# Layer 0 of a two-layer graph network: the weighted values of two source tiles as seven block products, each in its own PSUM bank

## The chip, the cores and the metric

One NeuronCore of a Trainium2 chip runs the whole program in one launch. The metric is device time in microseconds (us) from start to end of one execution. Engines are called as in the profile: PE (TensorE, its weight loads PEld), DVE (VectorE), ACT (ScalarE), POOL (GpSimd) and SP, whose queue issues most DMAs. Each engine takes its instructions in the written order, and what waits holds up all that stands behind it.

## The reference

Two layers over 4096 nodes with 512 features; `adj` is a 4096 x 4096 matrix of weights, about 1.6 % of them not zero. All arithmetic is float32.

```python
h = relu(layernorm(x))                       # layer 0
q, k, v = h @ Wq.T + bq, h @ Wk.T + bk, h @ Wv.T + bv
a = q @ k.T / sqrt(512) + adj + adj
x = x + softmax(a, axis=-1) @ v
h = relu(layernorm(x))                       # layer 1: 8 heads of 64 features
nX = a_ln * normalised(h @ W) + b_ln         # per head: mean and deviation over 64
kg = leaky_relu(at1 + at2.T, 0.2) * adj      # at1, at2: nX times a1, a2
y = softmax(where(adj != 0, kg, -32768)) @ nX + nX
x = x + elu(y)
```

## The kernel before

**Three phases.** The projections (layer norm, values `v`, queries times the key weights) fill the first 290 us. Layer 0's attention runs to about 2095 us. Layer 1 takes the rest. The change is in the first two.

**Tiles of layer 0.** Logits are held with sources on partitions and targets along the row. A *chunk* is 512 targets (`ic`, 8 of them), a *tile* one block of 128 sources by 512 targets (`jt`, 32 per chunk), and the loop handles a *pair* of tiles per round: 128 rounds, `s` counting tiles. In a round PE computes the scores of the next pair (s+2, s+3) and the weighted values of this one (s, s+1).

**Scores (`stage`, `product`, L740).** The scores of a pair are a 2 x 2 block matrix product, done with seven block products (Strassen's scheme in Winograd's form) of 128 x 256 outputs, each two matmuls deep, in four stages: stage 0 computes two products, stages 1 and 2 two each, stage 3 one. Their sums build up in three PSUM tiles, Z (one buffer) and X (two buffers). After each stage DVE adds Z or X onto the half tiles of `aT`, which hold the transposed adjacency (`add_part`, L748, 128x256 each, seven per pair); ACT takes exp of a whole tile in place (L753, after stages 2 and 3); POOL adds it onto `total`, the sum over sources (L758).

**Weighted values (`weighted`, L768).** For each tile and each of four blocks of 128 targets one matmul: 128 x 128 of the exponentials against 128 x 512 of `v`, accumulated over the 32 tiles of the chunk in four PSUM banks `acc0` to `acc3`. Eight per pair. PSUM has eight banks: four `acc`, two X, one Z, and one, `m`, that `small()` hands to the side jobs.

**Side jobs.** When a chunk ends, `chunk_end` divides its rows by their totals and adds `x`, and `make_ready` prepares them for layer 1 during the rounds of the next chunk: layer norm, four transposes per 128 rows (`turn`), the projection (`project`, four 512-column matmuls), deviations per head, attention coefficients, `sides` (small transposes) and `fours`. These jobs stand in a table `later`, keyed by step; the loop runs those that are due between the matmuls. In `m` they meet no score and no accumulator.

**Other work of a round.** DVE transposes two new adjacency tiles in 32 x 32 blocks (`swap`, L485) and writes mask and edge tiles for layer 1 (`for_layer_1`: `ng` L730, `gs` L732), which SP stores to DRAM. SP loads adjacency, hidden features (`hT`, `hS`) and, once per chunk, query tiles.

**Order.** All of this is put in program order by hand (`seq`); no scheduler moves it. Where one instruction needs another engine's result, or its buffer, the framework adds a semaphore wait; it tracks buffers by tile.

A round before, with PE's matmuls in this order: stage 0, `weighted` blocks 0 and 1, stage 1, blocks 2 and 3, side jobs, stage 2, three blocks of tile s+1, stage 3, the last block, side jobs. DVE's first swap and `for_layer_1` stand between the adds of stages 0 and 1, the second ones between those of stages 2 and 3.

Of the kernel before, what the change touches and what calls it, by code (L numbers as in the profile page):

```python
# [43 lines left out]
HUGE1 = 1e36  # L44

# [33 lines left out]
def fast_path(  # L79
# [50 lines left out]
    for t in (low0, high0):  # L130
        nc.vector.memset(t, 1.0)
# [4 lines left out]
    h_d = dram.tile([NS, P, KC, GC], F32, name="h_d")  # L136
    s_d = dram.tile([NS, P, 4, KC // 2, 2, P], F32, name="s_d")
    q_d = dram.tile([NI, P, KC, GC], F32, name="q_d")
    t_d = dram.tile([NI, P, 4, KC // 2, GC // 2], F32, name="t_d")
# [35 lines left out]
    def means(pool, rows, name):  # L175

        st = pool.tile([P, SB, 6], F32, name=f"{name}st", tag=f"{name}st", bufs=2)
        mv = pool.tile([P, SB, 2], F32, name=f"{name}mv", tag=f"{name}mv", bufs=2)
        for b in range(SB):
            seq(nc.vector.bn_stats(st[:, b, :], rows[b]))  # L180
            seq(nc.vector.bn_aggr(mv[:, b, :], st[:, b, :]))
        return mv
# [65 lines left out]
    def make_ready(ic, x1s, small, at_step, gap, last):  # L248

        n = SB * NH  # L250
# [5 lines left out]

        def features(b):
            return x1s[b].rearrange("p (h e) -> p h e", e=HD)

        def stats():  # L260
            state["mv"] = means(prep, x1s, "l")
# [19 lines left out]
        def turn():  # L281
            xn = state.pop("xn")
            m = small([P, KC, P])
            for k in range(KC):
                seq(nc.tensor.transpose(m[:, k, :], xn[:, ts(k, P)], ident))
            h1 = prep.tile([P, KC, P], F32, name="h1", tag="h1", bufs=1)
            seq(nc.scalar.activation(h1, m, AF.Relu))
            state["h1"] = h1

        def project():  # L290
            h1 = state.pop("h1")
            m = small([P, 2, GC] if last else [P, GC])
            y = m[:, 0, :] if last else m
            for k in range(KC):
                seq(nc.tensor.matmul(  # L295
                    y, h1[:, k, :], w1_sb[:, k].rearrange("p h e -> p (h e)"),
                    start=k == 0, stop=k == KC - 1,
                ))
            state["y"] = y
            if last:  # L300
                state["a"] = m[:, 1, 0 : 2 * NH]
                for k in range(KC):
                    seq(nc.tensor.matmul(
                        state["a"], h1[:, k, :], w1a_sb[:, k].rearrange("p e h -> p (e h)"),
                        start=k == 0, stop=k == KC - 1,
                    ))

        def keep_features(b):
            seq(nc.vector.tensor_copy(x1s[b], state.pop("y")))
            if last:  # L310
                seq(nc.vector.tensor_copy(
                    raw[:, b].rearrange("p e h -> p (e h)"), state.pop("a")
                ))
# [8 lines left out]

        def flat(t):
            return t.rearrange("p b h -> p (b h)")
# [11 lines left out]

        def root():
            v = flat(var)
            seq(nc.gpsimd.tensor_scalar(v, v, 1.0 / (HD - 1.0), 1e-30, ALU.mult, ALU.max))
            r = inverse_root(nc.gpsimd, prep, v, n, "s")  # L340
            seq(nc.gpsimd.tensor_mul(r, r, v))
            seq(nc.gpsimd.tensor_scalar_add(r, r, STD_EPS))
            state["r"] = r

        def inverse():
            seq(nc.vector.reciprocal(flat(var), state.pop("r")))
# [55 lines left out]
        def sides(b):  # L402
            r = ic * SB + b
            m = small([P, 4, P])
            for kind in range(4):
                seq(nc.tensor.matmul(
                    m[:, kind, :], parts[:, b, kind].rearrange("p h r -> p (h r)"),
                    ident_b, start=True, stop=True,
                ))
            zc = prep.tile([P, 4, P], BF16, name="zc", tag="zc", bufs=2)  # L410
            seq(nc.scalar.copy(zc, m))
            for g in range(2):
# [4 lines left out]
            nc.sync.dma_start(out=z1_d[:, :, ts(r, P)], in_=zc[:, 2:4, :])  # L417

        def fours():
# [3 lines left out]
            seq(nc.tensor.transpose(m, at1s.rearrange("p b h -> p (b h)"), ident))  # L423
# [6 lines left out]
        else:  # L430
            at_step(0, stats)
        at_step(0 if last else 1, deviations)
        for b in range(SB):
            d = (0 if last else 2) + gap * b
            at_step(d, norm, b)
            at_step(d + 1, turn)
            at_step(d + 2, project)
            at_step(d + 2, keep_features, b, late=True)
            at_step(d + 3, square, b)
            at_step(d + 3, variance, b, late=True)  # L440
            if last:
# [3 lines left out]
        if last:  # L445
            at_step(d + 6, ats)
            at_step(d + 6, split)
            for b in range(SB):
                at_step(d + 8 + b, sides, b)
                at_step(36 + 32 * b, own, b)  # L450
            at_step(d + 11, fours)
        else:
            at_step(d + 4, root)
            at_step(d + 6, inverse)
            for b in range(SB):
                at_step(d + 7 + b, products, b)
                at_step(d + 8 + b, sums_of, b)
                at_step(d + 12 + b // 2, own, b)
                at_step(d + 13 + b, sides, b)
            at_step(d + 11, split)  # L460
            at_step(d + 16, fours)
# [6 lines left out]
    with tc.tile_pool(name="early", bufs=2) as early, tc.tile_pool(name="kv", bufs=1) as kv:  # L468
# [26 lines left out]
        def load_chunk(ic, queue):  # L495
            loaded = []
            for k in range(KC):
                qt = early.tile([P, GC], F32, name="qt", tag="qt", bufs=16)
                seq(queue.dma_start(out=qt, in_=q_d[ic, :, k, :]))
                loaded.append(qt)  # L500
            for e in range(4):
                qt = early.tile([P, GC], F32, name="qt", tag="qt", bufs=16)
                seq(queue.dma_start(out=qt, in_=t_d[ic, :, e].rearrange("p k i -> p (k i)")))
                loaded.append(qt)
            queries_of[ic] = loaded
# [3 lines left out]
        def side_b(ic, name):  # L509

            q = queries_of[ic]
            if name[0] == "B":
                return [q[2 * (int(name[1]) - 1) + k][:, ts(int(name[2]) - 1, H)] for k in range(2)]
            return [q[3 + int(name[1])][:, ts(k, H)] for k in range(2)]

        def side_a(sb, pair, name):

            h, sums = hidden_of[sb]
            if name[0] == "A":
                tile_ = 2 * pair + int(name[1]) - 1  # L520
                return [h[:, 2 * (int(name[2]) - 1) + k, ts(tile_, P)] for k in range(2)]
# [11 lines left out]
        def load_hidden(sb):  # L533
            for t, ap in zip(hidden_tiles(sb), (h_d, s_d)):
                flat = "p a b -> p (a b)" if ap is h_d else "p a b c d -> p (a b c d)"
                seq(nc.sync.dma_start(out=t.rearrange(flat), in_=ap[sb].rearrange(flat)))


        with tc.tile_pool(name="proj_c", bufs=1) as pc, tc.tile_pool(
# [10 lines left out]
            bv_sb = early.tile([P, D], F32, name="bv_sb", tag="qt", bufs=16)  # L550
# [18 lines left out]
            def hidden(sb, xt):  # L569
# [17 lines left out]
                for t, ap in ((h, h_d), (sums, s_d)):  # L587
                    flat = "p a b -> p (a b)" if ap is h_d else "p a b c d -> p (a b c d)"
                    seq(nc.sync.dma_start(out=ap[sb].rearrange(flat), in_=t.rearrange(flat)))

            def values_of(sb):
                for b in range(SB):
# [6 lines left out]
                    seq(nc.vector.tensor_add(v[:, sb * SB + b, :], pv, bv_sb))  # L599

# [3 lines left out]
            def queries(sb):  # L604
                qs = pc.tile([P, KC, GC], F32, name="qs", tag="qs", bufs=1)
                for o in range(KC):
# [10 lines left out]
                seq(nc.sync.dma_start(  # L617
                    out=q_d[sb].rearrange("p k i -> p (k i)"), in_=qs.rearrange("p k i -> p (k i)")
                ))
                t = [  # L620
                    prep.tile([P, KC // 2, H], F32, name="ts", tag="x1", bufs=SB) for _ in range(4)
                ]
# [7 lines left out]
                for e in range(4):  # L630
                    seq(nc.sync.dma_start(
                        out=t_d[sb, :, e].rearrange("p k i -> p (k i)"),
                        in_=t[e].rearrange("p k i -> p (k i)"),
                    ))

# [67 lines left out]
        with tc.tile_pool(name="attn", bufs=2) as work, tc.tile_pool(  # L703
# [6 lines left out]

            def small(shape):
                return psum.tile(shape, F32, name="m", tag="m", bufs=1)

            def load_residual(ic):
                rows_of[ic] = []
                for b in range(SB):
                    x1 = prep.tile([P, D], F32, name="x1", tag="x1", bufs=SB)
                    nc.sync.dma_start(out=x1, in_=x[ts(ic * SB + b, P), :])
                    rows_of[ic].append(x1)
# [30 lines left out]
            def exponent0(s):  # L750
                ic, jt = TILES[s]
                p = turned.pop(s)
                seq(nc.scalar.activation(p, p, AF.Exp, scale=2.0))  # L753
                if jt == 0:
                    totals[ic] = work.tile([P, GC], F32, name="total", tag="total", bufs=2)
                    seq(nc.gpsimd.tensor_copy(totals[ic], p))
                else:
                    seq(nc.gpsimd.tensor_add(totals[ic], totals[ic], p))  # L758
                probs[s] = p

            def weighted(s, b):
                ic, jt = TILES[s]
                if jt == 0 and b == 0:
                    sums[ic] = [
                        psum.tile([P, D], F32, name=f"acc{b}", tag=f"acc{b}", bufs=1)
                        for b in range(SB)
                    ]
# [904 lines left out]
```

## Time and profile before

| what | us |
|---|---|
| median of three runs (3783.66 to 3793.55) | 3793.2 |
| the profiled execution | 3789.07 |
| its span, first to last instruction | 3787.3 |
| PE busy over the span | 3648.9 (96 %) |
| DVE, POOL, ACT busy | 2534.2, 2056.7, 1726.2 |
| layer 0's attention, 290 to 2090 us: PE, DVE, POOL, ACT busy of 1800 | 1770.0, 1039.6, 633.2, 230.9 |

Busy time counts an engine's instructions from start to end, overlaps once. A row of a timeline gives start, duration, engine, line, operation, operands and count of merged instructions; in brackets stands idle time before it and what ended that. A float32 matmul appears as two instructions (4 for a block product two deep), and a matmul's recorded duration overlaps the next one's: the spacing of starts says what it costs.

### The profile page before, as it was taken

To read this page: it belongs to the slowest core of one execution; us is meant where nothing else is said; L and a number is where in the kernel's file an instruction comes from. 1 tells how busy PE (TensorE), PEld (TensorE's weight loads), DVE (VectorE), ACT (ScalarE), POOL (GpSimd) and SP (SyncE) were. 2 spreads that over 40 slices of the span, in tenths; PEclk is the share of its full clock that TensorE was granted. 3 is DMA by queue.
4 is the path that set the end of the run, shared out by engine and by line. 5 is a ranking of instruction groups with operands and counts; after the bars stand their busy time and mean duration, and the time that the engine had idled before them with its cause. 6 is when DMAs were issued, how large, how long until landed. Compare 5 with 4: busy or idle time off the path is not lost. (4 is left out here: it accounts for less than half of the span.)

```text
span 3787.3 us, 53732 instructions
## 1 busy us (share of the span) xinstructions
PE 3648.9 (96%) x19722; PEld 1747.0 (46%) x19722; DVE 2534.2 (67%) x3875; ACT 1726.2 (46%) x1501; POOL 2056.7 (54%) x1348
## 2 busy tenths in 40 slices
PE   8999999999999999999999689999999999999998
PEld 3446666666666666666666222223323232222222
DVE  5535556556565565656655458888888888888787
ACT  1000011111111111111111379899999999998897
POOL 3432224325252242523415468888888888877786
PEclk9999999999999999999999799999999999999999
DMA  6466766858668675676856788877788887888775
GB/s 201 181 212 190 201 182 192 213 160 225 174 191 226 181 217 163 200 212 182 220 150 183 160 197 212 211 208 209 208 211 205 211 210 205 210 206 204 196 209 153
DMA packets 623041, 746.18 MB, mean 197 GB/s; under 512 B 84848, under 2 KB 468272, under 8 KB 603312
## 3 DMA queue, kind: packets, MB, share of 16 engines
q1 hardware_dynamic: 614896, 717.69, 68.1%
q0 software_dynamic: 6480, 23.60, 3.5%
q8 instruction: 156, 2.56, 0.3%
q10 hardware_dynamic: 1392, 1.38, 0.1%
q14 instruction: 117, 0.96, 0.1%
HBM read 562.43 MB, written 172.23 MB: 194 GB/s over the span
## 5 line engine op out<-in xcount | busy, mean ns | idle before, releaser
L1030 POOL TENSOR_TENSOR t<-t,g 128x1024 f32<-128x1024 f32 x512 | 1223.3, 2399 | 341.1 <-DVE t L1024 228.5
L1049 PE MATMUL acc<-t,nX 128*64 128x512 f32 x4096 | 1008.8, 609 | 0.0
L1037 ACT ACTIVATE t<-t 128x2048 f32<-128x2048 f32 (+1 forms) x527 | 976.5, 1853 | 0.6 <-POOL t L1030 0.5
L768 PE MATMUL acc<-v,aT 128*128 128x512 f32 x2048 | 963.2, 593 | 0.0
L758 POOL TENSOR_TENSOR total<-total,aT 128x512 f32<-128x512 f32 x248 | 340.4, 1372 | 1064.0 <-ACT aT L753 1051.8
L1024 DVE SCALAR_TENSOR_TENSOR t<-u,at2m,r 128x512 f32<-128x512 f32 x1024 | 719.2, 744 | 248.6 <-issue 143.8
L753 ACT ACTIVATE aT<-aT 128x512 f32<-128x512 f32 x256 | 161.2, 630 | 1323.1 <-DVE aT L748 1301.0
L1033 DVE TENSOR_TENSOR t<-l,g 128x1024 f32<-128x1024 f32 x512 | 623.6, 1218 | 22.9 <-DMA g<-gT_d 20.1
L992 ACT ACTIVATE l<-l 128x1024 f32<-128x1024 f32 x512 | 516.3, 1008 | 179.9 <-PE l L986 128.1
L768 PEld LDWEIGHTS acc<-v,aT 128*128 128x128 f32 x2048 | 390.1, 190 | 274.1 <-issue 246.0
L1049 PEld LDWEIGHTS acc<-t,nX 128*64 128x64 f32 x4096 | 248.0, 136 | 457.7 <-issue 450.9
L748 DVE TENSOR_TENSOR aT<-aT,X 128x256 f32<-128x256 f32 x512 | 214.9, 420 | 288.5 <-PE X L740 285.4
L748 DVE TENSOR_TENSOR aT<-aT,Z 128x256 f32<-128x256 f32 x384 | 159.6, 416 | 306.4 <-PE Z L740 301.7
L732 DVE SCALAR_TENSOR_TENSOR gs<-ng,aT 128x512 f32<-128x512 bf16 x256 | 279.4, 1091 | 9.8 <-DMA gT_d<-gs 1.1
L740 PE MATMUL Z<-qt,hS 128*128 128x256 f32 x1024 | 265.6, 382 | 8.4 <-DVE aT L748 8.4
L740 PE MATMUL X<-qt,hT 128*128 128x256 f32 x1024 | 264.6, 381 | 0.5 <-DVE aT L748 0.5
L740 PE MATMUL X<-qt,hS 128*128 128x256 f32 x1024 | 263.6, 380 | 0.0
L740 PEld LDWEIGHTS Z<-qt,hS 128*128 128x128 f32 x1024 | 192.9, 191 | 131.7 <-issue 56.9
L976 PEld LDWEIGHTS <-z 6*128 6x128 bf16 x2048 | 52.7, 91 | 429.5 <-DVE t L1024 337.7
L986 PE MATMUL l<-z_left,z 64*64 64x512 bf16 x2048 | 202.7, 383 | 49.4 <-DVE t L1033 16.7
L740 PEld LDWEIGHTS X<-qt,hT 128*128 128x128 f32 x1024 | 195.4, 191 | 81.9 <-issue 55.0
L1006 PE MATMUL r<-nx,ident_b 64*64 64x512 bf16 x1024 | 209.7, 403 | 3.0 <-DMA nx<-nT_d 3.0
(180 smaller groups left out, 3559.9 us busy)
## 6 DMA issues: line engine op xcount, KB each, us to landing
g<-gT_d SPq DMA_DIRECT2D x128, 1024.0 KB
ag<-in_adj_dram SPq DMA_DIRECT2D x256, 256.0 KB
hT<-h_d SPq DMA_DIRECT2D x64, 1024.0 KB
hS<-s_d SPq DMA_DIRECT2D x64, 1024.0 KB
gT_d<-gs SPq DMA_DIRECT2D x256, 256.0 KB
nb<-nT_d SPq DMA_DIRECT2D x128, 512.0 KB
nx<-nT_d SPq DMA_DIRECT2D x256, 256.0 KB
nT_d<-ng SPq DMA_DIRECT2D x256, 128.0 KB
```

Source lines behind the costliest of these rows:

```text
L732: seq(nc.vector.scalar_tensor_tensor(gs, ng, G_MASKED / NEG_BIG, aT, ALU.mult, ALU.add))
L740: seq(nc.tensor.matmul(out, a, b, start=start and k == 0, stop=k == 1, skip_group_check=not start,))
L748: seq(nc.vector.tensor_add(p, p, part))
L758: seq(nc.gpsimd.tensor_add(totals[ic], totals[ic], p))
L768: seq(nc.tensor.matmul(sums[ic][b], probs[s][:, ts(b, P)], v[:, jt, :], start=jt == 0, stop=jt == NB - 1))
L992: seq(nc.scalar.activation(lefts[n], lefts[n], AF.Relu, scale=4.0))
L1006: seq(nc.tensor.matmul(out[first + 2 * r][ts(c, HD), :], ident_b[rows, rows], masks[r != c][rows, jt % JB, :], start=False, stop=True, ski ...
L1024: seq(nc.vector.scalar_tensor_tensor(t[:, 2 + e, :], u4[:, e, :], at2m[:, jt, h : h + 1], right[e], ALU.max, ALU.add))
L1030: seq(nc.gpsimd.tensor_mul(t[:, 2:4, :], t[:, 2:4, :], both_heads(n)))
L1033: seq(nc.vector.tensor_mul(logits[n][:, 0:2, :], lefts.pop(n), both_heads(n)))
L1037: seq(nc.scalar.activation(t, t, AF.Exp))
L1049: seq(nc.tensor.matmul(grp["acc"][hf][ts(e, HD), :], nX[jt // SB][:, jt % SB, hg * HG + 2 * hf + e, :], t[:, hf + 2 * e, :], start=jt == 0 ...
```

## The change

The weighted values of a pair become a 2 x 2 block product too, done with seven products of 128 x 256 blocks. Of `A` (the pair's exponentials, in halves of 256 targets) POOL forms four sums per pair (`pair_sums`), and three adds per pair keep the totals; of `B` (the values, in halves of 256 features) the sums are formed once, in the projections: one takes the place of a half of `v`, and three per pair go to DRAM (`vt_d`) and are loaded in each round (`load_sums`). Each product accumulates over the chunk in a bank of its own, M1 to M7, with two 128-target halves in it. At a chunk's end one ACT copy and ten DVE adds combine the seven banks, in steps (`end()`) spread over two rounds.

Seven banks leave one. It is the tile XZ: Z is its first half, X its second, and `small()` gives the side jobs the Z half. What a side job left there is cleared by ACT (`zeros`, 128 x 256) before or after, as the slot asks. Side jobs run in three slots of a round: slot 0 after stage 3 of the round before, slot 1 after stage 0, slot 2 after stage 2; the jobs are cut to half a bank (`turn` and `project` into two parts, `sides` into two).

PE's order in a round is now: slot 0, products 1 and 7, stage 0, slot 1, products 2 and 4, stage 1, product 5, stage 2, slot 2, products 6 and 3, stage 3.

The residual `x` is added by an accumulating DMA on POOL's queue; ACT divides the rows. Query factors are stored as seven tiles of 256 KB per chunk. A fifth test at the end of the program asks that in each column of statistics the largest row total be at most 256 times the smallest, or the general path runs.

```diff
+            xz = psum.tile([P, 2, H], F32, name="XZ", tag="XZ", bufs=1)
             def small(shape):
-                return psum.tile(shape, F32, name="m", tag="m", bufs=1)
+                slot["used"] = True
+                if slot["n"] == 2:
+                    zeros()
+                m = xz[: shape[0], 0, 0 : math.prod(shape[1:])]
...
             def exponent0(s):
                 seq(nc.scalar.activation(p, p, AF.Exp, scale=2.0))
-                    seq(nc.gpsimd.tensor_add(totals[ic], totals[ic], p))
+            def pair_sums(s):
+                seq(nc.gpsimd.tensor_sub(s3, a11, a21))
+                seq(nc.gpsimd.tensor_add(s1, a21, a22))
+                seq(nc.gpsimd.tensor_sub(s2, s1, a11))
+                seq(nc.gpsimd.tensor_sub(s4, a12, s2))
...
+                    for t, a in ((total[0], a11), (total[0], a12), (total[1], s1)):
+                        seq(nc.gpsimd.tensor_add(t, t, a))
...
-            def weighted(s, b):
-                seq(nc.tensor.matmul(
-                    sums[ic][b], probs[s][:, ts(b, P)], v[:, jt, :], start=jt == 0, stop=jt == NB - 1
-                ))
+            def weighted(s, *which):
+                for i in which:
+                    a, b = factors[s][i]
+                    for u in range(2):
+                        seq(nc.tensor.matmul(
+                            sums[ic][i][:, u, :], a[:, ts(u, P)], b,
...
                 if n == 0:
-                    w["x"] = psum.tile([P, H], F32, name="X", tag="X", bufs=2)
-                    w["z"] = psum.tile([P, H], F32, name="Z", tag="Z", bufs=1)
+                    w["z"], w["x"] = xz[:, 0], xz[:, 1]
...
+                def divide(b):
+                    seq(nc.scalar.activation(
+                        x1s[b], x1s[b], AF.Identity, scale=rows_of[ic][:, b : b + 1]
+                    ))
+                def residual():
+                    seq(nc.gpsimd.dma_start(
+                        out=rows, in_=x[ts(ic, GC), :].rearrange("(b p) d -> p b d", p=P),
+                        accum_op=ALU.add,
+                    ))
+                    store_rows(ic, x1s)
...
+                parts_of_end = [
+                    then((copy, c11, m[1])),
+                    then((add, c22, c11, m[7])),
+                    then((add, c12, c11, m[5]), (add, c11, c11, m[2])),
+                    then((add, c21, c22, m[4]), (add, c22, c22, m[5])),
+                    then((add, c12, c12, m[6]), (add, c21, c21, m[6])),
+                    then((add, c22, c22, m[6]), (add, c12, c12, m[3])),
+                ]
+                at_step(s, 2, total_of_rows)
...
+                def hooks(n):
+                    slot.update(n=n, used=False)
+                    for f in later.pop(3 * (s // 2) + n, []):
+                        f()
+                    if n == 1 and slot["used"]:
+                        zeros()
...
+        for b in range(SB):
+            d = 8 + 6 * b
+            at_step(d, norm, b)
+            at_step(d + 1, turn, range(0, 2))
+            at_step(d + 2, turn, range(2, 4))
+            at_step(d + 3, project_half, b, 0)
+            at_step(d + 4, project_half, b, 1)
+            at_step(d + 4, square, b)
+            at_step(d + 5, variance, b)
+            at_step(d + 5, root_of, b)
...
+        for b in range(SB):
+            at_step(36 + 2 * b, sides, b, 0)
+            at_step(37 + 2 * b, sides, b, 1)
+            at_step(36 + 2 * b, own, b)
+        at_step(45, fours)
```

A step number counts three slots per round, from the first round of the next chunk.

## The prediction

> **What bounds the kernel now.** I read the busy table by stage first: in layer 0's attention (290 to 2090 us) PE is busy 1770 of 1800 us and the granted clock is 1.00. The list of PE's waits in that stretch holds 30 us in all, so the order of PE's matmuls sets the time. Then the timeline of PE alone, for one round without side jobs:
>
> ```profile
> 299.19 2.74 PE L768 MATMUL acc<-v,aT 128*128 128x512 f32 x6
> 301.77 1.03 PE L740 MATMUL X<-qt,hT 128*128 128x256 f32 x4
> 302.63 1.02 PE L768 MATMUL acc<-v,aT 128*128 128x512 f32 x2
> 303.49 1.03 PE L740 MATMUL Z<-qt,hT 128*128 128x256 f32 x4
> 304.35 1.03 PE L740 MATMUL X<-qt,hT 128*128 128x256 f32 x4
> 305.22 1.88 PE L768 MATMUL acc<-v,aT 128*128 128x512 f32 x4
> 306.93 1.03 PE L740 MATMUL Z<-qt,hS 128*128 128x256 f32 x4
> 307.80 1.03 PE L740 MATMUL X<-qt,hS 128*128 128x256 f32 x4
> 308.66 1.88 PE L768 MATMUL acc<-v,aT 128*128 128x512 f32 x4
> 310.38 1.03 PE L740 MATMUL Z<-qt,hS 128*128 128x256 f32 x4
> 311.24 1.03 PE L740 MATMUL X<-qt,hS 128*128 128x256 f32 x4
> 312.10 2.74 PE L768 MATMUL acc<-v,aT 128*128 128x512 f32 x6
> ```
>
> A round is 312.10 - 299.19 = 12.91 us, with no gap. Four 128x256 instructions (one block product) take 0.86 us from start to start, two of 128x512 also 0.86: the time goes by columns, 0.215 us per 256, and the weight loads hide. So 7 products (6.02) and 16 instructions of 512 columns (6.88) make 12.90.
>
> What a wait costs shows where PE does wait, in the first pair, before any weighted values fill the gaps:
>
> ```profile
> 285.84 1.03 PE L740 MATMUL X<-qt,hS 128*128 128x256 f32 x4
> 286.04 0.42 DVE L748 TENSOR_TENSOR aT<-aT,Z 128x256 f32<-128x256 f32 x1 [1.03 <-PE Z L740]
> 286.55 0.63 ACT L753 ACTIVATE aT<-aT 128x512 f32<-128x512 f32 x1 [55.58 <-DVE aT L748]
> 286.90 0.42 DVE L748 TENSOR_TENSOR aT<-aT,X 128x256 f32<-128x256 f32 x1 [0.44 <-PE X L740]
> 287.38 1.13 PE L740 MATMUL X<-qt,hT 128*128 128x256 f32 x4 [0.51 <-DVE aT L748]
> 288.35 1.03 PE L740 MATMUL Z<-qt,hT 128*128 128x256 f32 x4
> ```
>
> X's four end, by spacing, at 286.70; DVE starts its add 0.20 later, needs 0.42, and 0.06 after it PE starts again, on a group that takes 0.97 in place of 0.86, its first load being bare. PE end to DVE: 0.20. DVE end to PE: 0.06 + 0.11 = 0.17. ACT follows DVE by about 0.1.
>
> **Part 1, the products.** 16 instructions of 512 columns become 28 of 256 per round: 6.88 to 6.02, 0.86 less. X and Z show that 256-column instructions with a new weight each keep 0.215. 128 rounds: **-110 us**.
>
> **Part 2, one bank for Z and X.** The built program shows that waits on XZ are for the tile: the first product of each stage waits for the last add of the stage before, and the first add for the stage's last product. What must fit between two stages is 0.20, two adds, 0.17. Adds on different tiles start 0.33 apart where both are ready (296.12 and 296.45 in the timeline), on the same half 0.52 (293.45 and 293.97). Stages 0 to 1: 0.20 + 0.52 + 0.42 + 0.17 = 1.31, under two products (1.72). Stages 2 to 3: 1.12 under 1.72. Stage 3 to the next 0: one add, 0.79 under 1.72. Stages 1 to 2: 0.20 + 0.33 + 0.42 + 0.17 = 1.12 over product 5 alone, 0.86: PE stands 0.26 per round, 127 times: **+33**. The bounds are 0.2 and 0.5.
>
> **Part 3, the side jobs.** Before, `m` was free when they came; PE's waits for them sum to 13.5 us, all in `fours`. Now each writes the Z half directly after a stage, and PE, in order, waits for that stage's adds with nothing in between. The program has 84 such places in slot 0, 49 in slot 1 and 50 in slot 2: 26 per chunk in seven chunks, and the last `total_of_rows` stands after no stage but is counted too.
> - Slot 0, after stage 3: 0.20 + 0.42 + 0.17 = 0.79 if DVE is free. DVE comes from the second swap, `ng` and `gs` (0.70 + 0.43 + 0.69, with gaps 1.90), which starts 0.95 after stage 2's end; stage 3 ends 2.58 after it, so the add is ready at 2.78 and DVE free at 2.85, later where POOL's first subtraction holds it. I take 0.9: 84 x 0.9 = 76. Bounds 0.75 and 1.3.
> - Slot 1: two adds on one half, 1.31: 49 x 1.31 = 64. Bounds 1.2 and 1.6.
> - Slot 2: the clearing stands behind the exp: 0.20 + 0.42 + 0.10 + 0.63, then the clearing. No row has 128x256 on ACT; PSUM rows of 512 and 1024 columns take 0.59 and 1.01, so 0.82 ns a column and about 0.38. With 0.17 that is 1.90: 50 x 1.90 = 95. Bounds 1.1 (if exp does not come first) and 2.4.
> The matmuls of the jobs are as many columns as before. The jobs' readers (ACT or DVE, 0.4) hide under the two products that follow. Sum **+235**.
>
> **Part 4, DVE late.** DVE gets its first swap block after stage 0's adds, free 0.20 + 0.94 + 1.90 = 3.04 after stage 0; stage 1's adds are due at 3.64. A slack of 0.6 covers it, except where `variance` (0.68 and its wait) stands before: 28 rounds late by some 0.8, **+22**. POOL and DVE disturb each other: `gs` takes 0.69 alone and 1.64 beside a POOL add (mean 1.08). POOL's new work is seven adds of 256 columns per round; from 0.27 at 32 columns and 1.265 at 512, an estimate of 0.73 each, 5.1 us in place of 2.7. They run mostly before DVE's block; 0.15 us in 70 rounds, **+10** (0 to 30).
>
> **Part 5, the queues.** In round 0 of a chunk POOL's DMA of the residual waits for four ACT divisions (0.80 each, as `xn`), about 4.6 us after stage 2, and takes 0.9 to issue (L1093's rows); the next pair's first subtraction stands behind it, 0.73, so product 7 is due at 3.4 and gets its input at 6.5: 7 x 3.1 = **+22** (0 to 30). SP issues one more load per round (0.35 us of 12) and eight row stores that wait for that DMA; the edge stores behind them have a round's time. Traffic per round goes from 2.3 to 2.55 MB at 68 % share: hidden, 0 to 15 if not. A chunk's ten adds (0.69 each) are spread, and only the pair before stage 1 is late by 0.8: **+8** in all. The residual of the last chunk behind layer 0: **+5**. Projections: 64 POOL operations more (47 us on an engine busy 106 of 290): **+3**, up to 15. Layer 1 unchanged.
>
> **Sum.** -110 + 33 + 235 + 22 + 10 + 22 + 8 + 5 + 3 = +228, on the profiled 3789: 4017, and 4 more for the median of the runs: **4021**. The low ends (25; 63 + 59 + 55; 22; zeros) give +114, so 3907; the high ends (64; 109 + 78 + 120; 22 + 30 + 30; 38) give +381, so 4174.
>
> **A rule of the skill.** Idle clocks are the question here. The trace has PE idle 6.40 us at 280.77, and the 256-column instructions after it start 0.43 apart for some 3.5 us; after 1.96 us idle at 293.92 they keep 0.215. My longest regular stall is 1.9 us, so by the rows the clock holds. The Trainium skill ("TensorE: Matmul & The Clock Gate", section "A second HAM failure mode: psum-queue depth-cycling") says instead that a PE that micro-idles often between groups while it cycles through PSUM falls back to half clock again and again. By it, as an estimate, one window of 3.4 us at half speed for each of 183 stalls would add some 310 us.
>
> **Rivals.**
> 1. *Faster.* The bank waits are covered, and only the products count: -110 + 33 + 16 = 3728 (3680 to 3770). It needs a mean side-job stall under (110 - 33 - 16) / 183 = 0.33 us, less than one add (0.42). In order behind a stage, with 0.20 and 0.17 around the add, I see no way. 0.06.
> 2. *Slower than forecast by DVE.* POOL's adds hold `ng` and `gs` in every round: with 1.52 and 1.64 (both are in the trace) DVE is free at 5.0 instead of 3.04, 1.35 late in the 78 rounds without a slot-1 job: +105, 4125 (4090 to 4200). For it: POOL's share doubles. Against: its operations are half as long, and end as DVE's block begins. 0.13.
> 3. *Nothing.* Stalls about half as long (the jobs' waits being shared with waits that stand anyway): within 0.3 %, 0.02.
> 4. *The general path runs.* Row totals worked out from the inputs go from 50,012 to 1,123,661, a ratio of 22, within a column 12, under 256. 0.01.
> The forecast, stalls as summed, has 0.78.
>
> **How the numbers follow.** Three runs before spread by 0.26 %, so a difference of about 0.3 % can be told. The range 3890 to 4130 takes in the low ends and part of rival 2, and leaves out rival 1 and the far end. Faster 0.06, same 0.02, slower 0.92.
>
> **What would show it.** Right: `weighted` at 0.86 per two 128-column halves; PE idle before L259, L302 and L409 at some 0.8 to 1.9 us each, released by DVE's adds or ACT's clearing, 200 us and more in all; PE idle before stage 2 about 0.26 in every round; rounds without side jobs near 12.3 us. Wrong: idle before those lines under 0.4, a granted clock well below 1.00 in layer 0, `gs` at 1.6 in most rounds, or PE waiting for SP's loads.

## The result, and the profile after

| | before | after |
|---|---|---|
| median of the runs (us) | 3791.8 (3783.7 to 3793.6, 4 runs) | 4195.3 (4192.5 to 4201.3, 4 runs) |
| span of the profiled execution (us) | 3787.3 | 4194.0 |
| mean granted TensorE clock | 0.987 | 0.958 |
| layer 0's attention ends at (us) | 2095 | 2493 |

The change makes the kernel slower: the ratio is 1.107 (1.105 to 1.109). The direction was foretold; the forecast of 4021 (3890 to 4130) is 174 us too low, and the time lies outside the range.

The table by stage comes first. In the kernel after, its columns are the window, its length, busy time of PE, weight loads, DVE, ACT and POOL with their instructions, granted clock, DMA share and GB/s:

```profile
290.00:1000.00 710.00, 619.13 (x2679) 511.88 (x2680) 343.86 (x669) 89.79 (x165) 304.96 (x451) 0.95 0.65 183
1000.00:1700.00 700.00, 573.82 (x2432) 467.27 (x2431) 318.35 (x620) 96.03 (x189) 299.83 (x441) 0.93 0.62 173
1700.00:2400.00 700.00, 576.63 (x2457) 469.34 (x2456) 306.97 (x610) 95.87 (x186) 303.82 (x453) 0.94 0.59 165
```

PE was busy 98 % of this stage; now it is 84 %, and the clock, 1.00 before, is 0.93 to 0.95. Both are losses, and only the first was in the forecast.

A round without side jobs is as foretold. PE alone, from the timeline after:

```profile
677.20 1.03 PE L834 MATMUL M<-v,aT 128*128 128x256 f32 x4
...
684.10 1.03 PE L834 MATMUL M<-tv,aT 128*128 128x256 f32 x4
685.11 1.99 PE L782 MATMUL XZ<-qt,hS 128*128 128x256 f32 x8
686.94 1.89 PE L834 MATMUL M<-v,S 128*128 128x256 f32 x8
...
689.53 0.81 PE L834 MATMUL M<-v,aT 128*128 128x256 f32 x3
```

689.53 - 677.20 = 12.33 us, where it was 12.91. Fourteen products at 0.86 are 12.04; the other 0.29 is mostly the place between stages 1 and 2: 685.11 - 684.10 = 1.01 in place of 0.86, and 686.94 - 685.11 = 1.83 in place of 1.72 for the group behind it. What makes the kernel slow is in the other rounds. The list of PE's waits after (280 to 2480 us; sum, number of times, longest):

```profile
PE XZ L782 <- DVE aT L790: 97.2, 40, 7.9
PE XZ L259 <- DVE aT L790: 53.0, 56, 1.0
PE XZ L302 <- ACT XZ L742: 41.0, 28, 1.5
PE XZ L259 <- POOL at1s L426: 39.2, 6, 6.5
...
PE M L834 <- DMA tv<-vt_d: 23.8, 6, 5.2
...
PE M L834 <- POOL S L806: 18.5, 7, 2.8
```

The second and third lines are side jobs in the shared bank, which the prediction priced. Two of them:

```profile
655.34 1.89 PE L782 MATMUL XZ<-qt,hT 128*128 128x256 f32 x8
658.27 0.44 PE L259 MATMUL XZ<-ident,xn 128*128 128x128 f32 x2 [1.04 <-DVE aT L790]
...
673.83 1.03 PE L782 MATMUL XZ<-qt,hT 128*128 128x256 f32 x4
675.37 1.99 PE L302 MATMUL XZ<-w_sb,h 128*128 128x256 f32 x8 [0.51 <-DVE aT L790]
```

The brackets count from the recorded end of the matmul before, 0.17 us later than the next one could have started (1.03 recorded, 0.86 from start to start). By starts slot 1 loses 658.27 - 655.34 - 1.72 = 1.21, and slot 0 loses 675.37 - 673.83 - 0.86 = 0.68 and 0.11 in the group itself (677.20 - 675.37 = 1.83 in place of 1.72): 0.79.

The other four lines of the list are not side jobs that the prediction priced: a stage that waits 2 to 5 us for DVE, a transpose that waits 6.5 us for POOL, and products that wait for a load of `tv` or for POOL's block sum. Each has a place in the timeline of the kernel after.

**`sums_of` in slot 1.** DVE waits in it for POOL's `prod`, with stage 1's adds behind it:

```profile
696.76 2.48 POOL L363 TENSOR_TENSOR prod<-x,a_sb 128x512 f32<-128x512 f32 x2
...
698.06 0.69 DVE L367 TENSOR_REDUCE at<-prod 128x8 f32<-128x512 f32 x1 [4.00 <-POOL prod L363]
...
701.69 0.75 DVE L790 TENSOR_TENSOR aT<-aT,XZ 128x256 f32<-128x256 f32 x2
...
702.49 3.78 PE L782 MATMUL XZ<-qt,hS 128*128 128x256 f32 x8 [5.03 <-DVE aT L790]
```

DVE stands 4.00 us, then has to do its reductions, the swap, `ng` and `gs` before the adds, and PE stands 5.03. The eight matmuls behind it take 3.57 us from start to start (the next group starts at 706.06), not 1.72: they run at half the clock. (Such a stretch is called a half-clock spell below.)

**`fours`.** Its scaling on POOL stands behind six block-sum operations of the same round:

```profile
760.99 2.21 POOL L818 TENSOR_TENSOR total<-total,aT 128x256 f32<-128x256 f32 x3
763.28 0.30 POOL L426 TENSOR_SCALAR at1s<-at 128x32 f32<-128x32 f32 x1
...
763.63 0.39 PE L259 MATMUL XZ<-ident,at1s 128*32 128x128 f32 x1 [6.53 <-POOL at1s L426]
```

**The residual and the row stores.** POOL's DMA holds the first block difference, as foretold; but SP's eight row stores, which wait for that DMA, hold the next load of `tv`:

```profile
796.70 1.40 POOL L901 DMA_DIRECT2D x<-in_x_dram  x1 [9.34 <-ACT x L896]
...
798.92 2.07 PE L834 MATMUL M<-tv,S 128*128 128x256 f32 x4 [2.64 <-POOL S L806]
...
806.26 5.43 SPq L160 DMA_DIRECT2D x_d<-x  x8
...
816.93 0.40 SPq L756 DMA_DIRECT2D tv<-vt_d  x1
...
817.80 2.05 PE L834 MATMUL M<-tv,S 128*128 128x256 f32 x4 [4.66 <-DMA tv<-vt_d]
```

**Half clock.** Groups of four or more matmuls in the trace after that took 0.43 instead of 0.215 each, counted by their excess, come to some 90 to 100 us, in about 50 spells, most of 1.2 to 2.8 us. All but seven stand behind a wait of over 2 us, or behind the short wait that follows it. The seven stand behind the row totals: a wait of 1.45 us or a little more for the clearing, then eight matmuls of one column.

### The profile page after: what moved, and what is told of

It reads as the page before. It is cut to its first block, busy times and chain, and to the rows that moved or that the text cites. A ratio compares the mean times of both kernels' runs of the same rounds, so it can differ in the third digit from the quotient of the medians.

```text
span 4194.0 us, 59304 instructions
## 1 busy us (share of the span) xinstructions
PE 3714.1 (89%) x21482; PEld 2121.4 (51%) x21482; DVE 2499.2 (60%) x3966; ACT 1790.6 (43%) x1700; POOL 2430.1 (58%) x2223
## 5 line engine op out<-in xcount | busy, mean ns | idle before, releaser
L790 DVE TENSOR_TENSOR aT<-aT,XZ 128x256 f32<-128x256 f32 x896 | 353.4, 418 | 919.0 <-PE XZ L782 913.2
L782 PE MATMUL XZ<-qt,hS 128*128 128x256 f32 x2048 | 527.6, 403 | 97.7 <-DVE aT L790 96.3
L782 PEld LDWEIGHTS XZ<-qt,hS 128*128 128x128 f32 x2048 | 395.4, 198 | 201.5 <-DVE aT L790 148.8
L782 PE MATMUL XZ<-qt,hT 128*128 128x256 f32 x1536 | 395.2, 396 | 1.7 <-DVE aT L790 0.8
L782 PEld LDWEIGHTS XZ<-qt,hT 128*128 128x128 f32 x1536 | 310.2, 202 | 51.4 <-DVE qs L642 1.7
L834 PE MATMUL M<-v,aT 128*128 128x256 f32 x1024 | 272.2, 389 | 0.0
L818 POOL TENSOR_TENSOR total<-total,aT 128x256 f32<-128x256 f32 x360 | 258.7, 733 | 9.4
L834 PE MATMUL M<-tv,aT 128*128 128x256 f32 x1024 | 262.6, 379 | 0.0
L834 PE MATMUL M<-v,S 128*128 128x256 f32 x1024 | 255.9, 395 | 0.0
L834 PEld LDWEIGHTS M<-v,S 128*128 128x128 f32 x1024 | 202.5, 199 | 29.7
```

What stands on the lines that cost most here:

```text
L782: seq(nc.tensor.matmul(out, a, b, start=start and k == 0, stop=k == 1, skip_group_check=not start,))
L790: seq(nc.vector.tensor_add(p, p, part))
L818: seq(nc.gpsimd.tensor_add(t, t, a))
L834: seq(nc.tensor.matmul(sums[ic][i][:, u, :], a[:, ts(u, P)], b, start=jt == 0 and u == 0, stop=jt == NB - 2, skip_group_check=u == 1,))
```

## The experiments

Two theories. *Orders and clock:* the loss beyond the forecast is three orders of queues (the three places above) and the half-clock spells behind their long waits; what the prediction priced is right. *Bank:* one shared bank with its short waits in every round costs more than was priced, and lowers the clock by itself; the long waits would come back elsewhere when moved.

### One order at a time, and all three

`e1_sums_later`: the reductions go to slot 2 of the same round.

```diff
-            at_step(d + 8, sums_of, b)
+            at_step(d + 9, sums_of, b)
```

> The reductions of the attention products (sums_of) move from slot 1 to slot 2, behind stage 2's adds, so that DVE no longer waits for POOL's products ahead of stage 1's adds. Theory A (long waits, and half-clock spells after them): the idle time before stage 2 released by DVE falls from 88 us to under 20, and some 25 half-clock spells of about 1.8 us go with it: about -105 us, 4090. Theory B (the many short waits of 0.5 to 1.5 us lower the clock): only the idle time goes, about -68 us, 4127, granted clock in layer 0 as before near 0.94. If the DVE waits had another cause: no change, 4195.

Measured: 4096.2, 99 less. The waits of a stage for DVE fall from 89 us (without the 7.9 at the start) to 4, in 10 places. One knock-on: the split of the last block's sums now runs late, and the first job of the sides waits 4.5 us for it once a chunk (31.6 in all). PE's idle time in layer 0 fell by about 58 and the excess of the half-clock spells by about 35, which is nearly all of the 99.

`e2_fours_early`: the scaling alone goes three steps, one round, ahead of the transpose.

```diff
+        at_step(42, fours_of)      # at1s = 4 at, on POOL
         at_step(45, fours)         # transpose and copy
```

> POOL's scaling for fours is issued one round earlier, so that its transpose no longer stands behind six POOL operations of pair_sums. Theory A: the seven idle times of 6.5 us fall to 0.8 (-40 us) and one or two half-clock spells per chunk go (-15 to -27): about 4135. Theory B: -40 us, 4155.

Measured: 4134.4, 61 less, as *orders and clock* has it.

`e3_residual_late`: the residual's DMA goes one slot later, the row stores a round later, and the statistics follow.

```diff
-                at_step(s + 2, 2, residual)             # and store_rows at once
+                at_step(s + 2, 3, residual)
+                at_step(s + 2, 6, store_rows, ic, x1s)
-        at_step(5, stats, range(0, 2))
+        at_step(6, stats, range(0, 2))
```

> The accumulating DMA of the residual goes behind pair_sums on POOL's queue (next slot 0), the eight row stores one round later on SP's. Theory A: PE's waits for the loaded sums (24 us) and for POOL's sums (27 us) go, with two half-clock spells per chunk (-31): about 4113. Theory B: -51 us, 4144.

Measured: 4146.3, 49 less, near the second figure. The waits for `tv` and POOL's `S` are gone (51 us), but the statistics of all four blocks now stand in one step behind the residual's landing, and the waits of stages for DVE grow from 89 to 108. The next trace shows that place too.

`e4_all_three`: the three edits together.

> All three moves together; the side jobs and their 180 short waits stay where they are. Theory A: no wait over 2 us is left, the granted clock of layer 0 rises from about 0.94 to 0.99, time about 3940 (-255). Theory B: -160 us, about 4035, and the clock stays near 0.94.

Measured: 4001.0, 194 less, between the two figures; alone the three gave 99 + 61 + 49 = 209. The time is 20 us under the prediction's 4021. In the list of waits of this kernel (lines behind 426 are five higher, so L787 is L782) the jobs' waits are unchanged, and two waits of another origin stand:

```profile
PE XZ L787 <- DVE aT L795: 32.5, 19, 7.9
PE XZ L409 <- POOL parts L397: 31.6, 7, 4.5
```

The timeline shows what the first one is, the statistics behind the residual's load:

```profile
780.28 0.69 DVE L182 BATCH_NORM_STATS2 lst<-x 128x6 f32<-128x512 f32 x1 [3.25 <-DMA x<-in_x_dram]
...
784.38 3.47 PE L787 MATMUL XZ<-qt,hS 128*128 128x256 f32 x8 [2.92 <-DVE aT L795]
```

The clock in layer 0 is 0.97 to 0.99, with some 40 us of half-clock spells left in 20 places, 14 of them behind these two waits and six behind the row totals. None of the other 168 waits of side jobs, the longest of 1.8 us, has a spell behind it.

### What a side job costs, and where

`e5_between`: on top of e4, each slot's jobs stand between its two products.

```diff
-                hooks(0)
-                weighted(s, 1, 7)
+                weighted(s, 1)
+                hooks(0)
+                weighted(s, 7)
```

(and the same for slot 1 with 2, 4 and slot 2 with 6, 3.)

> The three moves of before, and the side jobs between the two products of their slot instead of ahead of them (slot 0 between products 1 and 7, slot 1 between 2 and 4, slot 2 between 6 and 3), so that 0.86 us of matmuls lie under each job's wait for the adds. Theory A (a job's wait is the add chain that the prediction summed, so one product under it takes 0.86 off each): slot 0 falls from 0.5 to 0.9 to nothing (77 jobs, about 54 us), slot 1 from 1.03 to 0.17 but its reader and the clearing (0.2 + 0.4 + 0.1 + 0.38 + 0.17 = 1.25) stick out of the one product behind it by 0.4 (49 jobs, 23 us saved), slot 2 from 1.45 to 0.6 (50 jobs, 43 us): 120 less than 4001, 3880 (3850 to 3905). Theory B (the job's reader, now under one product, holds the next stage by as much as the job saves): the idle moves from L259, L302 and L409 to the stage's first product, 3960 to 4000.

Measured: 3862.5, 139 less than e4, in the range of the first figure. The waits before L302 fall from 1.47 to 0.60 where they are for the clearing (0.86, one product); those before L259 fall from 56 of 0.95 to 28 of 0.18. The jobs' waits were what the prediction said, an add chain with nothing under it.

`e6_whole_bank`: jobs of 512 columns, in slot 0. The row totals go to slot 0 of the next round, and the transpose of `fours` stays in slot 1, at step 46.

```diff
-            at_step(d + 1, turn, range(0, 2)); at_step(d + 2, turn, range(2, 4))
-            at_step(d + 3, project_half, b, 0); at_step(d + 4, project_half, b, 1)
+            at_step(d + 1, turn)              # whole bank
+            at_step(d + 4, project_whole, b)
-            at_step(36 + 2 * b, sides, b, 0); at_step(37 + 2 * b, sides, b, 1)
+            at_step(36 + 3 * b, all_sides, b)
```

> On top of that, the side jobs take the whole bank (512 columns) and go into slot 0 alone, where a stage's end leaves both halves free: 14 jobs a chunk instead of 26; only the transpose of the fours stays in slot 1, and the row totals move to slot 0 of the next round. Theory A (each job costs by its place, not by its columns): slots 1 and 2 lose what is left of their waits (28 and 30 us) and some 0.2 each of bare loads (20 us), and the longer DVE reader of the features (0.7 in place of 0.42) takes some 6 us back: 3880 - 70 = 3810 (3780 to 3840). Theory B (the longer readers in slot 0 hold stage 0 as much): 3860 to 3880.

Measured: 3839.3, at the upper end of the first range; but that range counted from 3880, and of the 70 us that it named 23 came. The clearing's waits are gone; 15.1 us before L302 and 6.6 before the row totals are new, since in slot 0 these wait for DVE, whose second swap block stands before stage 3's add. And some 31 us of half clock stay, most behind the split (3.65 us, 7 times) and the statistics.

`e7_half`: half of product 6 goes into the place between stages 1 and 2.

```diff
                 weighted(s, 5)
+                weighted(s, 6, us=range(0, 1))
...
-                weighted(s, 6)
+                weighted(s, 6, us=range(1, 2))
```

> On top of that, half of product 6 (two matmuls, 0.43 us) moves from slot 2 to the place between stages 1 and 2, where the prediction's part 2 has PE standing 0.26 in each of 127 rounds. Theory A (part 2: the gap is the add chain of 1.12 over one product of 0.86): the gap closes, 33 us less than the run with whole banks, about 3775 (3750 to 3800). Theory B (the gap of 0.15 to 0.26 is a bare weight load that any group after a wait pays, or product 6's input is not there yet): 0 to 10 us.

Measured: 3862.2, 23 more. Both theories fell. Rounds without jobs go from 12.34 to 12.09, so the gap of part 2 is there and closes; but with 0.43 us less between stage 2 and slot 0, the jobs there wait that much longer for DVE's swap block (L302 0.72 to 0.95 in the mean, the transposes 0.18 to 0.47): idle rises from 88 to 126 us.

`e8_spread`: e7 with the statistics in two steps (6 and 7) and the first sides' job at steps 37 and 38.

> On top of that, two knock-ons of the moves are taken out: the statistics of two blocks each go into two steps instead of four blocks in one (the trace has PE idle 2.3 to 3.3 us there once a chunk), and the first job of the sides goes one and two slots later, as two half jobs, since POOL's split is not done (4.5 us idle once a chunk). Theory A (each of these waits costs its idle time, and the half-clock spell of about 1.8 us that follows one of over 2.3 us): 7 x (4.5 + 2.8 + 2 x 1.8) = 76 less, two more half jobs of 1.0 each a chunk, 14 more: about 60 less than the run before it, some 3715 (3690 to 3745), which would be faster than the kernel before the change. Theory B (the waits come back at the next job, and the half-clock spells stay, as many short waits alone cause them): 3760 to 3780.

Measured: 3865.9, no change. The wait for the split is gone at the job, and a product waits 4.64 us instead, 7 times, for POOL's first block difference, which stands behind the same split on POOL. A late consumer doesn't help where the producer's queue holds something else behind the same work.

### What a regular wait costs by itself

Four kernels put one pause into each of layer 0's 128 rounds of the kernel *before*:

```diff
                 weighted(s, 3)
+                pause(n)   # PE: 4 columns; ACT: 1 + n small copies in a chain; PE: 4 columns
```

> The kernel before the change with the pause of a chain of one and two copies on ACT, a wait of PE of about 0.9 us, some 1.4 us from the small matmul to the next full one. The longer pauses of 2.2, 3.2 and 4.3 us between the two cost 3.5, 5.2 and 6.9 us each. Theory A (there is a length below which the clock stays up, and the waits of under 1.2 us in the changed kernel are below it): 128 x 1.35 = 170, so 3955 (3935 to 3985), clock 1.00 in layer 0. Theory B (the spells come with a chance that falls with the length, and are still there): one wait in three with 1.8 us, 80 more, about 4035, clock about 0.96.

> The kernel before the change, with one wait of PE added in each of layer 0's 128 rounds, between the matmuls of 512 columns ahead of stage 2: a matmul of 4 columns into the side jobs' bank, a chain of one and five small copies on ACT that starts from it, and a matmul of 4 columns that waits for the chain. This measures by itself what a regular wait of a given length costs. By some 0.2 a copy the wait is about 1.5 us (1.2 to 1.9). Theory A (the clock follows the length of a single wait; none of under about 2 us lowers it): the time grows by 128 waits, some 190 us, 3980, and the clock in layer 0 stays 1.00. Theory B (many short waits lower the clock as well): 128 x 1.8 more, some 4200, with the clock at 0.9 or below.

> The same with a chain of one and eight copies, a wait of about 2.2 us (1.8 to 2.7). Theory A: 128 x 2.2 = 280 for the waits, and a half-clock spell of 1.8 us behind part of them (14 of 22 in the trace after the change): 60 % of 128 gives 140 more, some 4210, clock about 0.93 in layer 0. Theory B (every wait, also the shorter one, is followed by a spell): 280 + 230, 4300. A third outcome, that no spell follows, as after the 1.96 us at the start of the kernel before: 4070.

> The same with a chain of one and twelve copies, a wait of about 3.1 us (2.5 to 3.7). Theory A: a spell behind nearly every wait (27 of 31 in the trace after the change for waits of over 2.5): 128 x 3.1 = 400, and 128 x 1.8 = 230, some 4420, clock about 0.88 in layer 0. If waits cost no more than themselves, 4190.

| run | first small matmul to the next full one (us) | time, over before (us) | per pause (us) | clock in layer 0 | pauses with a spell behind |
|---|---|---|---|---|---|
| e15_pause2 | 1.39 | 3962.3, +179 | 1.40 | 1.00 | none of 128 |
| e11_pause5 | 2.21 | 4228.8, +446 | 3.49 | 0.92 to 0.93 | 102 of 128 |
| e12_pause8 | 3.24 | 4452.6, +670 | 5.23 | 0.88 | 124 of 128 |
| e13_pause12 | 4.35 | 4670.2, +888 | 6.93 | 0.85 to 0.86 | 128 of 128 |

The last column counts rounds whose matmuls behind the pause took over 1 us more than 0.215 us per 256 columns. A pause in the timeline of e15, and the matmuls behind it at 0.43 per 512 columns (3.54 us for eight):

```profile
612.10 0.39 PE L844 MATMUL m<-idle_t,ident 128*128 128x4 f32 x2 [0.80 <-ACT idle_t L843]
612.55 3.70 PE L295 MATMUL m<-w_sb,h 128*128 128x512 f32 x8
616.09 1.03 PE L742 MATMUL Z<-qt,hS 128*128 128x256 f32 x4
```

And one of e11, where four of 256 columns take 1.71 us from start to start, twice 0.86:

```profile
623.41 0.39 PE L844 MATMUL m<-idle_t,ident 128*128 128x4 f32 x2 [1.68 <-ACT idle_t L843]
...
624.76 1.91 PE L742 MATMUL Z<-qt,hS 128*128 128x256 f32 x4
626.47 1.44 PE L742 MATMUL X<-qt,hS 128*128 128x256 f32 x4
```

Shown: a regular pause of 1.4 us costs itself; one of 2.2 us costs 1.3 us more, in the mean, and one of 4.4 us 2.6 more. So the clock half of the *bank* theory falls, but for the row totals: 128 pauses of about the size of the jobs' waits do not lower the clock. The three longer pauses came out above what was expected (e11 beside its second figure, so that alone it would have spoken for the *bank* theory; e12 and e13 above both of theirs). For this pause the spells set in between 1.4 and 2.2 us, and a recorded wait of 1.68 is already beyond that. That the few columns around it count for little is the likely reason; no run varies them alone.

It is not a limit for every wait. The profile before has spells behind two of its four waits for `hT` of 1.65 to 1.91 us, and none behind the three of 2.20, 2.44 and 2.62. The 1.93 us ahead of the transpose of `fours` has none in seven places there and seven in e15. One of the two waits with a spell:

```profile
683.89 1.13 PE L740 MATMUL Z<-qt,hT 128*128 128x256 f32 x4 [1.88 <-DMA hT<-h_d]
684.86 1.80 PE L740 MATMUL X<-qt,hT 128*128 128x256 f32 x4
686.45 2.84 PE L768 MATMUL acc<-v,aT 128*128 128x512 f32 x4
```

Here 686.45 - 684.86 = 1.59 where 0.86 is usual. What decides between such waits stays open.

### Is it the order of the queues to the end

`e10_half_four`: from e6, the split behind slot 0's block sums, the statistics in steps 6 and 7, and half of product 4 (whose place has 1.72 us for a chain of 1.31) between stages 1 and 2.

```diff
-        at_step(35, split)
+        at_step(36, split)             # first sides at 38 and 40, as two halves
-                weighted(s, 4)
+                weighted(s, 4, us=range(1))
...
                 weighted(s, 5)
+                weighted(s, 4, us=range(1, 2))
```

> From the kernel with whole banks (3839): POOL's split goes one slot later, behind the block sums of slot 0 instead of ahead of them, and the first sides' job follows as two half jobs in slots 2 and 1; the statistics go into two steps; and the place between stages 1 and 2 gets half of product 4 instead of half of product 6, so that slot 0 keeps its two products. Theory A (POOL's and DVE's order was what those waits stood for, and between stages 0 and 1 the adds need 1.31 of the 1.72 that lie there): the wait for the split (25 us) goes, the one for the statistics falls from 3.3 to some 1.4 (13), half-clock spells with them (16), two half jobs more a chunk cost 9, the gap of 0.25 closes in 127 rounds (32): 3839 - 77 = 3762 (3740 to 3785), a little faster than the kernel before the change. Theory B (DVE is by now the bound of a round: its swap block, due 0.43 earlier, holds stage 1's adds): the gap comes back ahead of stage 1, 3795 to 3815.

Measured: 3801.6, 38 less than e6: the second figure, but not by its cause, since the stages' waits for DVE fall from 40 to 26 us. What stays is POOL again: 16.2 us of waits for `S` (7 of 2.3) and 13.8 for the split. Which of the four moves gave how much is not separated.

`e14_own_apart`: `own` of the four blocks at steps 33, 39, 42, 45, the first sides at 40 and 41.

> From the run of 3802: POOL's rows of the layer's own features (two operations of 1.27 us a block) leave the steps in which the block sums wait behind them (`own` goes to slot 0 of four different rounds), and the first sides' job waits two slots more for POOL's split. The trace of that run has PE idle 2.3 us before product 7 (POOL's sums behind two `own`) and 2.0 before the sides, once a chunk each, and 12 to 17 us of half-clock spells. Theory A (what is left of the loss is POOL's order): 7 x 2.3 + 7 x 2.0 + about 9 of spells = 39 less, 3763 (3750 to 3780), faster than the kernel before by about half a per cent. Theory B (the waits come back elsewhere, since DVE and POOL are full in those rounds): 3790 to 3805.

Measured: 3816.1, above both figures. The last `own`, read from the tile that the next chunk's end writes, now stands in front of that chunk's first copy on ACT, and a stage waits 3.0 us for a clearing behind it; the one at step 33 stands before a block sum (1.9 us).

`e16_own_early`: `own` at steps 24, 30, 39, 42.

> The run of 3816 had moved POOL's rows of own features (`own`) into slot 0 of four rounds, of which the last stood behind the end of the chunk (the copy of the next chunk's product 1 waited for it, PE 3.0 us) and one ahead of a block sum (1.9 us, once a chunk). Here they stand in slot 0 of rounds 8, 10, 13 and 14 of a chunk, in which POOL's row shows no product of features. Theory A (order of POOL alone): 7 x 3.0 + 7 x 1.9 + about 12 of half-clock spells less than 3816, some 3770 (3755 to 3783), at or just under the kernel before the change. Theory B (POOL is full in any round, another job's operands come late instead): 3795 to 3815.

Measured: 3760.6 (3759.2 to 3767.2, 5 runs) beside 3778.9 for the kernel before: 0.9959 (0.9945 to 0.9973), 0.4 % or 18 us less. Its stage table has the clock back:

```profile
290.00:1000.00 710.00, 689.09 (x3093) 568.99 (x3092) 408.20 (x784) 99.15 (x166) 366.69 (x526) 1.00 0.77 220
1000.00:1700.00 700.00, 675.87 (x3017) 547.64 (x3016) 395.57 (x773) 106.04 (x179) 396.61 (x578) 1.00 0.76 215
1700.00:2060.00 360.00, 347.34 (x1543) 280.75 (x1542) 193.77 (x378) 55.30 (x95) 213.37 (x309) 1.00 0.71 203
```

Half-clock spells are down to 2, and PE's waits in layer 0 (without the 7.9 us at the start) to 58 us. DMA is at 0.71 to 0.77, where the change had 0.59 to 0.65, and PE waits for loads in one place: transfers were not the limit. Layer 0 ends at 2062 us, 32 before the old end. So with the jobs' places and POOL's order made for them the kernel with seven products comes out a little ahead. Not shown is how much of that the products give: the kernel before kept its own 28 us of waits, for `hT` and in `fours`, and no run mends those there. That waits come back elsewhere when moved, the last part of the *bank* theory, held in e4, e8 and e14, and ended with e16.

## Why the prediction was wrong

By its own terms, in the profiled execution (span 4194.0 against 3787.3, 407 us):

| term | foretold | measured |
|---|---|---|
| part 1, products | -110 | 0.86 a product, as foretold |
| part 2, stage 1 to 2 | +33 | 0.25 to 0.29 a round, some 25 in the rounds without a longer wait there |
| part 3, side jobs' waits | +235 | 174 idle, some 211 by starts, without `fours` |
| part 4, DVE late | +22 and +10 | 89, in 39 places, by another cause |
| part 5, POOL's queue | +22 | 27 |
| part 5, SP's stores, "a round's time" | 0 | 24 |
| `fours` | inside part 3 | 45 |
| clock | 0 | 90 to 100 |
| waits of the kernel before that are gone (`hT`, its `fours`) | 0 | -28 |

With -110, and some 10 more by starts for the 61 waits counted as idle, these come to 383 to 393 of the 399 us by which layer 0 ends later (2493.2 against 2094.6). What follows takes 8 us longer.

**Right:** parts 1 and 2, to 0.03 us of a round. Part 3 was right too, within a tenth: by starts slot 0 measured 0.74 to 1.03, slot 1 1.20 to 1.26, slot 2 1.67 to 1.75 (medians), against 0.9, 1.31 and 1.90; e5 showed that the mechanism was the named one. Rival 1 fell, since no wait was hidden. Rival 2's mechanism fell as well: `gs` takes 793 ns in the mean after, less than the 1082 before.

**The step that failed first is part 4**, with its sentence that the slack of 0.6 "covers it, except where `variance` (0.68 and its wait) stands before". What it priced there is at most 4 us, the waits that e1 left; what it left out is 85. It followed DVE's own operations and the port, but not the step `sums_of`, which the changed kernel has in slot 1 and whose DVE half waits for a POOL half issued in the slot before, 2.5 us of `prod` behind a scaling and three sums. In part 5, "the edge stores behind them have a round's time" checked the stores and not the `tv` load, which is new, small and due in every round. And `fours` was priced as a job that waits for adds, without POOL's queue before it. All three were moved steps whose other engine's queue wasn't walked.

**The second is the clock.** "My longest regular stall is 1.9 us, so by the rows the clock holds" failed twice: the stalls were up to 6.5 us, by the missing terms, and the row it rests on (1.96 us idle at the start of the kernel before, no spell) was one sample. The same profile has spells behind waits of 1.88 and 1.91 us, named above, and the pause of 2.2 us was followed by one in 102 of 128 rounds. With the three orders mended (e4) the time was 4001, 20 under the forecast. That it lies so near is in part luck: e4 still has some 100 us that the forecast lacked (42 of half clock, 32 for the split, 25 of stages' waits), and lacks the 62 of parts 4 and 5 and the 28 us of old waits.

**The rule weighed there.** In the runs, 128 pauses of 1.4 us left the granted clock at 1.00, and the 2.2 us ones took it to 0.92 to 0.93. The Trainium skill ("TensorE: Matmul & The Clock Gate", section "A second HAM failure mode: psum-queue depth-cycling") warned of a clock that falls by frequent short idles; here the long ones did it, and of the short waits of the shared bank only the row totals. Its section "Why this matters for your kernels" puts the limit of a gap at about 3 us; for the regular pause measured here it is shorter, between 1.4 and 2.2, and the measurement decides for this case. The prediction's estimate by the rule, 310 us for 183 stalls, was the wrong size on the wrong stalls; the 90 to 100 us came from about 50.

## What to carry to other kernels

When work is moved between slots, walk every moved step through each engine that it touches, and ask at each queue what stands behind it: a two-engine step (POOL multiplies, DVE reduces) put one slot early cost 99 us, a store that waits for a DMA cost the loads behind it. Price a PE wait in two parts, its length, and, from some 2 us on, the half clock that may follow it (1.3 to 2.6 us in the mean behind the regular pauses here). One independent product put between a dependent pair took up to its 0.86 us off each wait (e5). Compare waits by starts: the idle time in brackets was 0.17 us short. Before giving up a spare PSUM bank, put the small jobs that lived there under a product and in the one slot where the bank is free: that alone moved 4001 to 3839.

## What the runs showed of the hardware that was not expected

The clock's answer to a regular pause has a step: nothing at 1.39 us, a spell that costs 1.8 us (median) behind 102 of 128 pauses at 2.21, one behind 124 of 128 at 3.24 and behind all at 4.35, where it costs 2.8 us. For single waits the length alone does not say it: 2.62 us passed without a spell, 1.88 did not. Matmuls of one column seem not to keep the clock up: in e4's trace six of the seven row totals, with waits of about 1.5 us, have a spell behind them, and none of the 28 waits of 1.45 us ahead of the 256-column matmuls of L302. And DVE was disturbed less than the prediction feared: beside POOL's 256-column operations of 0.73 us, `gs` takes 793 ns in the mean, where 1082 had stood beside the longer ones.
